# Layer 3 of a fused four-layer convolution kernel: row sums on VectorE, one mask operation for four heads, and other orders of columns in PSUM

## The chip, the cores and the metric

The kernel runs on one core of a Trainium2 chip. The metric is the device time of one execution in microseconds (us); a kernel's time is the median of its runs. Engines are named as in the profile: PE is the matmul engine, PEld its weight load, DVE is VectorE, ACT is ScalarE, POOL is GpSimd, SP is SyncE, whose queue issues nearly all DMAs in order.

## The reference, cut to what matters

The input `x` has 4 images of 256 channels, 48 x 48 pixels. Four layers follow each other, each of the form `x = x + layer(groupnorm(x))`. Layers 0 to 2 are convolutions, which the change does not touch. Layer 3 is a linear attention over boxes of pixels. It has 8 heads of 32 channels and three window sizes:

```python
q = sigmoid(Wq x); k = sigmoid(Wk x); v = (Wv x) / |Wv x| per head and pixel
Ik  = cumsum over rows and columns of k
Ikv = the same of the outer product of k and v
for w in (1, 2, 4):                      # boxes of side 48, 24 and 12
    wk, wkv = box(Ik), box(Ikv)          # sums of k and of k*v over the box around a pixel
    norm = sum_d q_d * wk_d
    outs.append((sum_d q_d * wkv_d) / (norm + 1e-6))
out = Wout concat(outs) + bout
```

A box sum is a difference of prefix sums along the columns and along the rows.

## The kernel before, in words

All of it is one program. A helper class `InOrder` records every operation in the order in which Python issues it, so nearly all rows of the profile carry the one line L244 and are told apart by tile names. Layers 0 to 2 fill the first 1390 us or so; the projections of layer 3 for image 0 already run in their shadow. Layer 3 is the rest.

**Blocks and tiles.** Layer 3 works through 48 blocks: 4 images, 2 halves of the channels (`ct`, four heads each), 6 blocks of 8 pixel rows (`rb`). A block goes through 8 to 12 score tiles; there are 480 in all. For a tile, `scores` computes on PE the products of queries and keys of four heads into two PSUM tiles `s` (a pair of heads each). `masked` makes the window masks of it in SBUF tiles `sm`: ACT and DVE write the widest window (a relu; PE has added large negative numbers where the window does not reach), DVE multiplies the middle window by a 0/1 mask, and POOL multiplies DVE's result by the mask of the narrowest window. `sums` multiplies the three with the values `vs` on PE, into three accumulators `acc`, one for each window. `LAG = 2`: while PE computes scores of tile n it sums tile n-2. Columns inside a block are stored `(w r)`: the pixel's column first, its row in the block of 8 second. Sums of a finished block are copied by ACT into `stage`.

**Norms.** A second path computes the denominators.
- `qk` projects q and k, takes the sigmoid on ACT into `sg`, and stores q in column order (`q_d`), k in two orders (`k_d` by way of a second tile `kt`, and `kf_d` in row order).
- `k_sums` runs twice side by side, once for each half of the channels, over 4 x 6 blocks of rows (48 steps in all). It loads the keys of 8 rows into `kp`, a tile with gaps of zeros between the rows, sums along the columns with two scans on DVE (`cs`), subtracts two shifted views for each window on DVE (`pt`), and then sums down the rows on POOL: eight adds of 3 windows x 48 columns, and a copy of the last row into `carry`. The result goes to DRAM (`kb_d`).
- `norms` loads two such rows of sums (`nhi`, `nlo`) and the queries (`nq`), and on POOL subtracts and multiplies, the queries read by a rearranged view. PE sums over the channels of each head into `norm_ps` (row order); ACT copies it into `ns`. It goes through DRAM (`n_d`, `nr`, the reciprocal on DVE, `r_d`).
- `prepare` loads the reciprocals, spread over channels, into `rc`, and POOL multiplies the first half's sums `o` by them. `finish` does the same for the second half on DVE (`stage`), multiplies by `Wout` on PE into `out_ps`, and DVE adds bias and residual into `res`. Both reciprocal products read `rc` by a rearranged view, and the addition of the residual writes `res` by one.

**What sets the order.** The side jobs (`qk`, `k_sums`, `norms`, `prepare`, `finish`, states of whole key blocks) are Python generators. After every tile `advance` lets them take steps. A planner gives each tile a budget of PE time and of POOL time: `pool_turn` holds a job back until the POOL budget allows it, by the cost `pool_op(n) = 190 + 1.95 n` ns; the budget of a tile is 3600 ns less `far_time`, the cost of its own narrow masks. Since all queues are in order, a side job that comes late on POOL holds up what stands behind it: mask products on POOL, loads on SP, norm matmuls on PE.

Of the kernel before, what the change touches and what calls it, by code (L numbers as in the profile page):

```python
# [247 lines left out]
def conv_preact_kernel(  # L248
# [71 lines left out]
    q_d = [dram.tile([C, HW], F32, tag=f"q{b}", name=f"q_d{b}") for b in range(B)]  # L320
    k_d = [dram.tile([C, HW], F32, tag=f"k{b}", name=f"k_d{b}") for b in range(B)]
# [105 lines left out]
    class Projection:  # L427
# [50 lines left out]
        def qk(self, g, a, name, mo):  # L478
            b = self.b
            while g not in self.xn:  # L480
                if g in self.left:
                    return
                yield 1
            yield from take("kt")
            yield from bank(1, NCT * product_time(NB))
            ps = self.ps_tile()[:, 0:NB]
            for ct in range(NCT):
                self.product(
                    ps,
                    proj[name][:, ct, mo * P : (mo + 1) * P],  # L490
                    self.xn[g][:, ct],
                    start=(ct == 0),
                    stop=(ct == NCT - 1),
                )
            self.used(g)
            t = self.scr.tile([P, NB], F32, tag="sg", name="sg")
            if name == "q":
                rows = t.rearrange("p (c x r) -> p c r x", c=NKC, x=KC)
            else:
                rows = t.rearrange("p (r c x) -> p c r x", c=NKC, x=KC)  # L500
            act.activation(
                rows, ps.rearrange("p (c r x) -> p c r x", c=NKC, x=KC), AF.Sigmoid
            )
            chans, cols = slice(mo * P, (mo + 1) * P), slice(a * NB, (a + 1) * NB)
            if name == "k":
                kt = self.scr.tile([P, NB], F32, tag="kt", name="kt")
                act.copy(kt.rearrange("p (c r x) -> p c r x", c=NKC, x=KC), rows)
            yield 1
            if name == "k":
                sync.dma_start(out=k_d[b][chans, cols], in_=kt)  # L510
            sync.dma_start(out=(q_d if name == "q" else kf_d)[b][chans, cols], in_=t)
            free["kt"] += 1
            made.add((name, b, mo, a))
# [1108 lines left out]
    with (  # L1622
# [4 lines left out]
        tc.tile_pool(name="smp", bufs=2 * (LAG + 1), reuse_waits="tile") as smp,  # L1627
# [27 lines left out]
        GAP = HALVES[0] + 1  # L1655
# [5 lines left out]
        carry = wts.tile([P, NCT, NW, W], F32, name="carry")  # L1661
# [10 lines left out]
        def k_sums(mo):  # L1672
# [14 lines left out]
            for at, (b, a) in enumerate(todo):  # L1687
# [3 lines left out]
                while step < loaded + FETCH + 1:  # L1691
                    yield 1
                yield from take("cs")
                cs = scr.tile([P, (RB + 1) * ROW], F32, tag="cs", name="cs", bufs=1)
                n = GAP + RB * ROW
                for i, j in ((0, n // 2), (n // 2, n)):
                    dve.tensor_tensor_scan(
                        cs[:, i:j],
                        kp[:, i:j],
                        kp[:, 0:1].to_broadcast([P, j - i]),  # L1700
                        cs[:, i - 1 : i] if i > 0 else 0.0,
                        ALU.add,
                        ALU.add,
                    )
                    yield 1
# [4 lines left out]
                for wi, h in enumerate(HALVES):  # L1710
                    dve.tensor_sub(pt[:, wi], shifted(cs, h - 1), shifted(cs, -h - 1))
                    yield 1
                free["cs"] += 1
                for r in range(RB):
                    if r % 2 == 0:
                        yield from pool_turn(NW * W, 2)
                    if a > 0 or r > 0:
                        up = pt[:, :, r - 1, :] if r > 0 else carry[:, mo]
                        pool.tensor_add(pt[:, :, r, :], pt[:, :, r, :], up)
                pool.tensor_copy(carry[:, mo], pt[:, :, RB - 1, :])  # L1720
                yield 1
# [8 lines left out]
        def norms(b, rb):  # L1730
# [4 lines left out]
            def load(ct):  # L1735
# [3 lines left out]
                qf = scr.tile([P, W, RB], F32, tag="nq", name="nq")  # L1739
                sync.dma_start(  # L1740
                    out=qf.rearrange("p w r -> p (w r)"),
                    in_=q_d[b][chans, rb * NB : (rb + 1) * NB],
                )
# [28 lines left out]
            for hi, lo, qf in loaded:  # L1772
                for wi, h in enumerate(HALVES):
                    n = min(RB, max(0, h + 1 - rb * RB))
                    if n < RB:
                        yield from pool_turn((RB - n) * W)
                        pool.tensor_sub(hi[:, wi, n:RB], hi[:, wi, n:RB], lo[:, wi, n:RB])
                for wi in range(NW):
                    yield from pool_turn(NB)
                    pool.tensor_mul(hi[:, wi], hi[:, wi], qf.rearrange("p w r -> p r w"))  # L1780
                sums.append(hi)
# [3 lines left out]
            for ct in range(NCT):  # L1785
# [3 lines left out]
                for wi in range(NW):  # L1789
                    pe.matmul(  # L1790
                        ps[D * wi : D * (wi + 1), 0:NB],
                        head_sel[:, ct, :],
                        sums[ct][:, wi].rearrange("p r w -> p (r w)"),
# [97 lines left out]
        class Block:  # L1891
# [48 lines left out]
            def masked(self, a, half, ss):  # L1940
# [9 lines left out]
                def room():  # L1950

                    t = smp.tile([P, SM_ROOM], F32, tag="sm", name="sm")
                    at, blocks_, views = 0, {}, {}
                    for wi in wis:
                        y0, y1 = rows_seen(wi, a, rb)
                        ps = self.parts(wi, a, half)
                        if wi == 0:
                            n = sum(p1 - p0 for _, p0, p1 in ps) * (y1 - y0)
                            block = t[:, at : at + 2 * n].rearrange("p (j n) -> p j n", j=2)
                            blocks_[wi] = block  # L1960
                            at, o = at + 2 * n, 0
                            for c, p0, p1 in ps:
                                m = (p1 - p0) * (y1 - y0)
                                views[wi, c] = block[:, :, o : o + m].rearrange(
                                    "p j (x r) -> p j x r", r=y1 - y0
                                )
                                o += m
                            continue
                        for c, p0, p1 in ps:
                            n = 2 * (y1 - y0) * (p1 - p0)  # L1970
                            views[wi, c] = t[:, at : at + n].rearrange(
                                "p (j x r) -> p j x r", j=2, r=y1 - y0
                            )
                            at += n
                    assert at <= SM_ROOM
                    return blocks_.get(0), views

                pairs = [room() for _ in ss]

                def times_mask(engine, wi, c, rows, cols, dst, src):  # L1980
# [5 lines left out]
                        dst, src, m.unsqueeze(1).to_broadcast([P, 2, ncol, nr])  # L1986
# [4 lines left out]
                def middle(s, room_):  # L1991
                    y0, y1 = rows_seen(1, a, rb)
                    for c, p0, p1 in parts_seen(1, half):
# [4 lines left out]
                        times_mask(dve, 1, c, (y0, y1), (p0, p1), room_[1][1, c], src)  # L1998

                def widest(engine, s, room_):  # L2000
                    n = room_[0].shape[2]
                    lo, hi = strip_columns(half) if full else (0, n)
                    if engine is act:
                        act.activation(room_[0], s[:, :, lo:hi], AF.Relu)
                    else:
                        dve.tensor_scalar_max(room_[0], s[:, :, lo:hi], 0.0)

                first, second = zip(ss, pairs)
# [8 lines left out]
                if many:  # L2017
                    (y0, y1), (z0, _) = rows_seen(2, a, rb), rows_seen(1, a, rb)
                    seen1 = {c: p0 for c, p0, _ in parts_seen(1, half)}
                    for _, views in pairs:  # L2020
                        for c, p0, p1 in parts_seen(2, half):
                            src = views[1, c][
                                :, :, p0 - seen1[c] : p1 - seen1[c], y0 - z0 : y1 - z0
                            ]
                            times_mask(pool, 2, c, (y0, y1), (p0, p1), views[2, c], src)
                return [views for _, views in pairs]
# [24 lines left out]
            def sums(self, wi, a, half, sms):  # L2051
# [3 lines left out]
                for k, (c, p0, p1) in enumerate(self.parts(wi, a, half)):  # L2055
                    for j in range(HG):
# [5 lines left out]
                            sms[j // 2][wi, c][:, j % 2],  # L2062
# [24 lines left out]
        def prepare(i):  # L2087
# [26 lines left out]
            for wi in range(NW):  # L2114
                yield from pool_turn(NB)
                ow = o[:, wi].rearrange("p (w r) -> p w r", w=W)
                pool.tensor_mul(ow, ow, rcs[0][:, wi].rearrange("p (r w) -> p w r", w=W))
# [4 lines left out]
        def finish(i, stage):  # L2122
# [13 lines left out]
            def divide(wi):  # L2136
                sw = stage[:, wi].rearrange("p (w r) -> p w r", w=W)
                dve.tensor_mul(sw, sw, rc[:, wi].rearrange("p (r w) -> p w r", w=W))
# [3 lines left out]
            for mo in range(NCT):  # L2142
                yield from bank(HOLD, NCT * product_time(NB))
                ps = ps_m.tile([P, 512], F32, tag="st", name="out_ps")[:, 0:NB]
                for wi in range(NW):
# [6 lines left out]
                    for t in range(NCT):  # L2152
                        kt = wi * NCT + t
                        tiled(
                            ps,
                            wout_sb[:, kt, mo * P : (mo + 1) * P],
                            os[t][:, wi, :],
# [4 lines left out]
                if mo == 0:  # L2162
                    free["rc"] += 1
                xs = res[:, mo].rearrange("p r w -> p w r")
                dve.scalar_tensor_tensor(
                    xs, ps.rearrange("p (w r) -> p w r", w=W), bout_sb[:, mo : mo + 1], xs, ALU.add, ALU.add
                )
# [111 lines left out]
        def far_time(i, a, half):  # L2279
# [4 lines left out]
            return 2 * sum(pool_op(2 * n) for n in columns(NW - 1, a, half, rb))  # L2284
# [79 lines left out]
```

## Time and profile before

| what | value |
|---|---|
| median of 3 runs | 3273.11 us (3265.43 to 3276.16) |
| the profiled execution | 3273.94 us, span 3272.1 us |
| mean granted PE clock | 0.955 of full speed |
| busy: PE, PEld | 2902.1 us (89%), 2004.4 us (61%) |
| busy: DVE, ACT, POOL | 2017.0 us (62%), 963.2 us (29%), 1613.6 us (49%) |
| instructions on DVE, ACT, POOL | 3907, 1894, 2658 |

The span runs from the first to the last instruction of the profiled execution. A row of a group reads: line, engine, operation, output tile <- input tiles, the most frequent shape of output <- input (and how many other shapes the group mixes), xcount | busy us in all, mean ns of one | idle us of the engine just before them, and what ended most of it. A row of the timeline gives the start, the duration, engine, operation and count, and in brackets the idle time before and what ended it. In rows of PE an f32 matmul counts twice, as it runs in two instructions.

### The profile page before, as it was taken

Reading aid. Unit: us, or ns where it says so; the run is one execution under the profiler, and the core shown is the slowest. Engines: PE = TensorE matmul, PEld = TensorE weight load, DVE = VectorE, ACT = ScalarE, POOL = GpSimd, SP = SyncE. Lnnn points to the kernel's source line nnn. Section 1 sums busy time; section 2 is a strip of 40 time slices with the busy share of each in tenths; the row PEclk is TensorE's granted clock in tenths of the full one; section 3 lists DMA queues with packets and bytes.
Section 4 is the critical chain, followed back from the end, with each engine's and each line's share of the span. In section 5 each row is a group of like instructions: output and inputs, shape, how many; then the busy total and the mean of one; then the engine's idle time right before and its main releaser. Section 6 shows DMA issues by size and latency. Waiting matters only on the chain.

```text
span 3272.1 us, 98025 instructions
## 1 busy us (share of the span) xinstructions
PE 2902.1 (89%) x41802; PEld 2004.4 (61%) x41802; DVE 2017.0 (62%) x3907; ACT 963.2 (29%) x1894; POOL 1613.6 (49%) x2658
## 2 busy tenths in 40 slices
PE   3678999899899978889986879998999999999999
PEld 2456777678677756756553536564656655666665
DVE  7886578648856632656675636665556665655555
ACT  0002210111121053245431224442335532333332
POOL 0000021003002130358999968989857888844554
PEclk9889899999999978989998989999999999999999
DMA  8746513332341243144554645354543354511322
GB/s 269 222 152 186 168 47 128 112 121 83 103 155 57 90 148 121 61 128 131 170 173 136 178 145 160 118 170 138 159 123 126 126 162 149 164 40 41 87 75 68
DMA packets 373126, 424.46 MB, mean 130 GB/s; under 512 B 129075, under 2 KB 328531, under 8 KB 371539
## 3 DMA queue, kind: packets, MB, share of 16 engines
q1 hardware_dynamic: 371491, 416.32, 41.1%
q8 instruction: 331, 5.42, 0.7%
q0 software_dynamic: 144, 1.08, 0.2%
q14 instruction: 104, 0.85, 0.1%
q10 hardware_dynamic: 1056, 0.79, 0.1%
HBM read 287.91 MB, written 131.25 MB: 128 GB/s over the span
## 4 chain that ended last, share of the span: by engine, by line
PE 51%; POOL 16%; DVE 10%; DMA 3%; ACT 3%; issue 3%; SPq 1%; ACTq 0%; POOLq 0%; DVEq 0%
PE cv L244 15%; PE s L244 13%; PE acc L244 11%; POOL sm L244 6%; PE out_ps L244 5%; PE proj_ps L244 4%; POOL nhi L244 4%; POOL pt L244 3%; PE ap L244 2%; DVE sm L244 2%; DVE l2v L244 2%; ACT sm L244 2%; SPq L244 1%; DVE v L244 1%; POOL vu L244 1%
## 5 line engine op out<-in xcount | busy, mean ns | idle before, releaser
L244 DVE TENSOR_TENSOR sm<-s,masks 128x448 f32<-128x448 f32 (+11 forms) x1536 | 632.6, 468 | 443.7 <-PE s L244 417.3
L244 POOL TENSOR_TENSOR sm<-sm,masks 128x352 f32<-128x352 f32 (+11 forms) x1024 | 685.9, 702 | 363.9 <-DVE sm L244 263.1
L244 ACT ACTIVATE sm<-s 128x384 f32<-128x384 f32 (+2 forms) x864 | 470.5, 545 | 845.3 <-PE s L244 662.2
L244 PE MATMUL acc<-sm,vs 128*32 128x128 f32 (+20 forms) x17920 | 626.1, 279 | 36.4 <-POOL sm L244 31.7
L244 PE MATMUL cv<-vx,wt 128*128 128x288 f32 x2080 | 562.8, 427 | 88.6 <-DVE vx L244 50.3
L244 PE MATMUL s<-qs,ks 32*128 32x192 f32 (+3 forms) x7680 | 594.3, 401 | 41.6 <-ACT sm L244 36.3
L244 PEld LDWEIGHTS acc<-sm,vs 128*32 128x32 f32 x17920 | 431.6, 110 | 241.9 <-issue 139.0
L244 PEld LDWEIGHTS s<-qs,ks 32*128 32x128 f32 x7680 | 372.7, 186 | 271.1 <-issue 122.3
L244 PEld LDWEIGHTS cv<-vx,wt 128*128 128x128 f32 x2080 | 404.7, 199 | 211.3 <-issue 52.7
L244 POOL MEMSET v<- 128x16 f32 (+1 forms) x120 | 18.7, 216 | 744.7 <-DVE vx L244 628.3
L244 PE MATMUL cv<-v,wl 128*128 128x384 f32 x1152 | 226.4, 357 | 25.2 <-DVE x L244 8.1
L244 PEld LDWEIGHTS cv<-v,wl 128*128 128x128 f32 x1152 | 216.4, 197 | 36.4 <-issue 16.7
L244 DVE TENSOR_SCALAR sm<-s 128x896 f32<-128x896 f32 (+1 forms) x96 | 111.1, 1157 | 186.1 <-PE s L244 161.2
L244 POOL TENSOR_TENSOR pt<-pt 128x144 f32<-128x144 f32 x336 | 188.0, 560 | 25.2 <-DVE pt L244 1.0
L244 POOL TENSOR_TENSOR nhi<-nhi,nq 128x384 f32<-128x384 f32 x144 | 176.2, 1243 | 0.0
L244 PE MATMUL s<-masks 24*128 24x192 bf16 (+2 forms) x1920 | 172.1, 269 | 0.0
L244 POOL TENSOR_TENSOR v<-l2v,v 128x384 fp32r<-128x384 f32 x96 | 109.0, 1166 | 117.4 <-ACT v L244 108.7
L244 PE MATMUL cv<-pad,wl 128*128 128x384 bf16 x864 | 145.6, 331 | 4.2 <-ACT pad L244 4.2
L244 PE MATMUL out_ps<-o,wout_sb 128*32 128x384 f32 x1152 | 123.8, 499 | 7.4 <-DVE res L244 3.4
L244 PE MATMUL out_ps<-stage,wout_sb 128*32 128x384 f32 x1152 | 123.5, 498 | 6.2 <-DVE stage L244 6.2
L244 PEld LDWEIGHTS <-wl 128*128 128x128 bf16 x864 | 84.5, 98 | 64.7 <-issue 7.2
L244 DVE SCALAR_TENSOR_TENSOR res<-out_ps,bout_sb,res 128x384 f32<-128x384 f32 x48 | 42.1, 878 | 128.9 <-PE out_ps L244 128.8
(174 smaller groups left out, 3515.1 us busy)
## 6 DMA issues: line engine op xcount, KB each, us to landing
wt<-wt SPq DMA_DIRECT2D x48, 768.0 KB
kb_d<-pt SPq DMA_DIRECT2D x48, 576.0 KB
rc<-r_d SPq DMA_DIRECT2D x192, 144.0 KB
nhi<-kb_d SPq DMA_DIRECT2D x120, 192.0 KB
nlo<-kb_d SPq DMA_DIRECT2D x88, 192.0 KB
o_d<-stage SPq DMA_DIRECT2D x24, 576.0 KB
o<-o_d SPq DMA_DIRECT2D x24, 576.0 KB
wl<-wl_d SPq DMA_DIRECT2D x16, 768.0 KB
```

Source lines behind the costliest of these rows:

```text
L244: return lambda *args, **kwargs: self.tc.keep_in_program_order(op(*args, **kwargs))
```

## The change

Four edits, all in layer 3:

1. `k_sums` sums down the rows first, on DVE and in place in `kp` (eight adds of 48 columns, and a copy of the last row into `carry`, which no longer has a window dimension). The scan multiplies the running sum by a tile `inside` that is 0 at the start of each row and 1 elsewhere, so that the sum starts anew in each row. The first columns of each window's result, where the window is cut at the border, are copied by ACT; the others are subtracted on DVE. The store follows at once, without a pause of a step.
2. `masked` gives the four heads of a tile one SBUF tile `sm` (3 buffers of double size instead of 6), and POOL multiplies the narrowest window of all four heads in one operation for each column part. `far_time` is adapted.
3. `qk` also stores q in row order (`qr_d`), by way of a copy on ACT into `kt`. `norms` loads this one, and multiplies without rearranging.
4. PE writes `norm_ps` in column order, through a rearranged view of its output, and `out_ps` in row order likewise. With this `rc`, `o`, `stage` and `res` are read and written without rearranged views.

The core of the diff:

```diff
@@ qk
-            if name == "k":
-                kt = self.scr.tile([P, NB], F32, tag="kt", name="kt")
-                act.copy(kt.rearrange("p (c r x) -> p c r x", c=NKC, x=KC), rows)
+            kt = self.scr.tile([P, NB], F32, tag="kt", name="kt")
+            pattern = "p (r c x) -> p c r x" if name == "q" else "p (c r x) -> p c r x"
+            act.copy(kt.rearrange(pattern, c=NKC, x=KC), rows)
...
+            first, second = (qr_d, q_d) if name == "q" else (k_d, kf_d)
+            sync.dma_start(out=first[b][chans, cols], in_=kt)
+            sync.dma_start(out=second[b][chans, cols], in_=t)
@@ set-up of layer 3
-        GAP = HALVES[0] + 1
+        GAP = HALVES[0]
...
+        inside = wts.tile([P, (RB + 1) * ROW], F32, name="inside")
+        nc.gpsimd.memset(inside, 1.0)
+        for r in range(RB + 1):
+            nc.gpsimd.memset(inside[:, r * ROW + GAP - 1 : r * ROW + GAP], 0.0)
@@ k_sums
+                keys = shifted(kp, 0)
+                for r in range(RB):
+                    if a > 0 or r > 0:
+                        up = keys[:, r - 1] if r > 0 else carry[:, mo]
+                        dve.tensor_add(keys[:, r], keys[:, r], up)
+                    if r % 4 == 3:
+                        yield 1
+                dve.tensor_copy(carry[:, mo], keys[:, RB - 1])
...
                     dve.tensor_tensor_scan(
                         cs[:, i:j],
+                        inside[:, i:j],
                         kp[:, i:j],
-                        kp[:, 0:1].to_broadcast([P, j - i]),
                         cs[:, i - 1 : i] if i > 0 else 0.0,
-                        ALU.add,
+                        ALU.mult,
                         ALU.add,
                     )
...
-                    dve.tensor_sub(pt[:, wi], shifted(cs, h - 1), shifted(cs, -h - 1))
+                    ahead_, behind_ = shifted(cs, h - 1), shifted(cs, 0)
+                    act.copy(pt[:, wi, :, : h + 1], ahead_[:, :, : h + 1])
+                    dve.tensor_sub(
+                        pt[:, wi, :, h + 1 :], ahead_[:, :, h + 1 :], behind_[:, :, : W - h - 1]
+                    )
                     yield 1
                 free["cs"] += 1
-                for r in range(RB):
-                    if r % 2 == 0:
-                        yield from pool_turn(NW * W, 2)
-                    if a > 0 or r > 0:
-                        up = pt[:, :, r - 1, :] if r > 0 else carry[:, mo]
-                        pool.tensor_add(pt[:, :, r, :], pt[:, :, r, :], up)
-                pool.tensor_copy(carry[:, mo], pt[:, :, RB - 1, :])
-                yield 1
@@ norms
-                    pool.tensor_mul(hi[:, wi], hi[:, wi], qf.rearrange("p w r -> p r w"))
+                    flat = hi[:, wi].rearrange("p r w -> p (r w)")
+                    pool.tensor_mul(flat, flat, qf)
...
-                        ps[D * wi : D * (wi + 1), 0:NB],
+                        ps[D * wi : D * (wi + 1), 0:NB].rearrange("p (w r) -> p r w", w=W),
@@ masked
-                    for _, views in pairs:
-                        for c, p0, p1 in parts_seen(2, half):
-                            src = views[1, c][
-                                :, :, p0 - seen1[c] : p1 - seen1[c], y0 - z0 : y1 - z0
-                            ]
-                            times_mask(pool, 2, c, (y0, y1), (p0, p1), views[2, c], src)
+                    for c, p0, p1 in parts_seen(2, half):
+                        src = views[1, c][:, :, p0 - seen1[c] : p1 - seen1[c], y0 - z0 : y1 - z0]
+                        times_mask(pool, 2, c, (y0, y1), (p0, p1), views[2, c], src)
@@ prepare
-                ow = o[:, wi].rearrange("p (w r) -> p w r", w=W)
-                pool.tensor_mul(ow, ow, rcs[0][:, wi].rearrange("p (r w) -> p w r", w=W))
+                pool.tensor_mul(o[:, wi], o[:, wi], rcs[0][:, wi])
@@ finish
-                sw = stage[:, wi].rearrange("p (w r) -> p w r", w=W)
-                dve.tensor_mul(sw, sw, rc[:, wi].rearrange("p (r w) -> p w r", w=W))
+                dve.tensor_mul(stage[:, wi], stage[:, wi], rc[:, wi])
...
-                            ps,
+                            ps.rearrange("p (r w) -> p w r", w=W),
                             wout_sb[:, kt, mo * P : (mo + 1) * P],
-                            os[t][:, wi, :],
+                            os[t][:, wi, :].rearrange("p (w r) -> p w r", w=W),
...
-                xs = res[:, mo].rearrange("p r w -> p w r")
-                dve.scalar_tensor_tensor(
-                    xs, ps.rearrange("p (w r) -> p w r", w=W), bout_sb[:, mo : mo + 1], xs, ALU.add, ALU.add
-                )
+                xs = res[:, mo].rearrange("p r w -> p (r w)")
+                dve.scalar_tensor_tensor(xs, ps, bout_sb[:, mo : mo + 1], xs, ALU.add, ALU.add)
@@ far_time
-            return 2 * sum(pool_op(2 * n) for n in columns(NW - 1, a, half, rb))
+            return sum(pool_op(4 * n) for n in columns(NW - 1, a, half, rb))
```

## The prediction

> **What bounds the kernel now.** Read the page's row of busy tenths first: layer 3, which the change touches, fills the span from about 1392 us on, with PE mostly at 9 and POOL mostly at 8 or 9 until about 2850 us. Which of the two sets the pace is told by cutting layer 3 into eight stretches of 60 score tiles each (equal attention work; eight batch halves). The cuts follow from the trace's score matmuls: 960 `s<-qs,ks` and 240 `s<-masks` per stretch. The view of busy time by stretch (us, then busy us and count for PE, PEld, DVE, ACT, POOL, then clock, DMA share, GB/s):
>
> ```profile
> 1392.20:1619.80 227.60, 213.49 (x4717) 137.76 (x4717) 144.61 (x295) 112.08 (x224) 180.66 (x340) 0.95 0.46 142
> 1619.80:1894.20 274.40, 229.07 (x4442) 135.43 (x4442) 174.64 (x305) 75.85 (x152) 255.36 (x362) 0.96 0.56 164
> 1894.20:2157.80 263.60, 238.14 (x4750) 139.85 (x4750) 145.55 (x288) 108.43 (x215) 216.41 (x352) 0.95 0.46 138
> 2157.80:2397.60 239.80, 218.56 (x4476) 134.58 (x4476) 138.94 (x264) 76.88 (x155) 208.35 (x301) 0.96 0.55 161
> 2397.60:2623.30 225.70, 221.02 (x4784) 135.76 (x4780) 140.33 (x284) 111.21 (x222) 167.31 (x326) 1.00 0.38 117
> 2623.30:2849.60 226.30, 212.38 (x4387) 133.87 (x4382) 134.86 (x258) 72.36 (x144) 197.94 (x271) 0.98 0.56 164
> 2849.60:3049.30 199.70, 186.89 (x4112) 127.84 (x4108) 104.78 (x215) 69.81 (x138) 96.39 (x155) 1.00 0.15 46
> 3049.30:3272.10 222.80, 210.78 (x4324) 131.50 (x4320) 117.77 (x235) 68.09 (x132) 114.37 (x162) 1.00 0.27 79
> ```
>
> The like stretches 3 and 5 (263.6 and 225.7 us, nearly the same PE count) and 2, 4 and 6 (274.4, 239.8, 226.3) differ by up to 48 us. The slow ones have the longest POOL time (255 us in stretch 2, 93%) and a lower clock (0.95 to 0.96 against 1.00)[...]. What PE waited for in layer 3, us in total, times, longest:
>
> ```profile
> PE s L244 <- ACT sm L244: 36.3, 94, 1.9
> PE acc L244 <- POOL sm L244: 31.7, 52, 2.1
> PE norm_ps L244 <- POOL nhi L244: 29.5, 18, 10.8
> PE norm_ps L244 <- DMA nhi<-kb_d: 8.6, 1, 8.6
> ...
> ```
>
> POOL stands behind most of it. The 10.8 us gap shows how, in the timeline: POOL's late `o` products free `rc`, SP's in-order queue waits there with its `rc` loads, the next norms' loads are issued behind them, POOL itself runs dry, and PE stands at its norm matmuls.
>
> ```profile
> 1911.96 2.33 POOL L244 TENSOR_TENSOR o<-o,rc 128x384 f32<-128x384 f32 x2
> ...
> 1914.70 2.12 SPq L244 DMA_DIRECT2D rc<-r_d  x3
> ...
> 1920.12 0.43 SPq L244 DMA_DIRECT2D nq<-q_d  x1
> ...
> 1925.31 0.99 POOL L244 TENSOR_TENSOR nhi<-nhi,nlo 128x384 f32<-128x384 f32 x1 [11.01 <-DMA nlo<-kb_d]
> ...
> 1928.97 3.77 PE L244 MATMUL norm_ps<-nhi,head_sel 128*32 128x384 f32 x6 [10.77 <-POOL nhi L244]
> ```
>
> So PE is the floor and POOL is what keeps the kernel off it until 2850 us.
>
> [...] partial-row `acc` matmuls that write 3 of every 8 columns start every 100 ns per eight at 57 columns (1.75 ns a column), the contiguous ones every 112 ns at 64 (1.75). [...] 1243 ns (`nhi*nq`) and 1244 ns (`o*rc`) with one operand strided, 1039 ns (`nhi-nlo`) with none, at 128x384. [...] the fastest `pt<-cs` took 541, the mean 743 beside POOL.
>
> **The change, part by part.** Groups of the page and of the trace by form carry these; counts after the change are those of the built order.
>
> (1) Row sums go from POOL to DVE, before the scan, on one copy of the keys instead of three windows.
>
> ```profile
> L244 POOL TENSOR_TENSOR sm<-sm,masks 128x352 f32<-128x352 f32 (+11 forms) x1024 | 685.9, 702 | 363.9 <-DVE sm L244 263.1
> ...
> L244 POOL TENSOR_TENSOR pt<-pt 128x144 f32<-128x144 f32 x336 | 188.0, 560 | 25.2 <-DVE pt L244 1.0
> L244 POOL TENSOR_TENSOR nhi<-nhi,nq 128x384 f32<-128x384 f32 x144 | 176.2, 1243 | 0.0
> ```
>
> POOL loses 188 us, 40 adds with `carry` at 543 ns (22) and 48 copies at 380 ns (18): -228. DVE gains 376 adds and 48 copies of 128x48. No such row exists; the line through DVE's `sm` rows (267 ns at 114, 619 at 448) gives 197 ns at 48[...]. I take 0.2 us: +85 (bounds 60 to 130, for a dependent chain). The scan keeps 2 x 300 elements (0.98 us each); its second operand is now a tensor instead of a broadcast, taken as equal, bound +-0.2 us x96. The three subtractions of 384 (743 ns) shrink to 184, 280 and 328 elements: [...], so -45. ACT copies the edges, 200, 104 and 56 elements: from `state` 238 ns at 96 and `kt` 512 at 384 about 0.34+0.25+0.20, times 48: +38. What queues behind the adds: they come in fours (0.8 us) between two tiles' mask products on DVE, which hold 2.2 us of a 3.5 us tile, so they fit; two key streams at once fill the tile. The store `kb_d<-pt` now follows its last subtraction directly, so SP's queue waits for DVE up to about 2 us, 48 times, in place of POOL.
>
> (2) One POOL operation for both pairs: 1024 become 512 of double size. The fixed part, from the means (518 ns at 130, 961 at 352: 2.0 ns per element), is 258 ns, from the medians (472, 886) 230. 512 x 0.235 = -120. The first now waits for both pairs' DVE products, about 1.1 us later than the first pair's, but PE takes both pairs of one column part before the next part, so it starts after one of two operations instead of three of four; two tiles of lag (7 us) cover it.
>
> (3) Rows and columns. `nhi*nq` and `o*rc` become contiguous: 0.2 us x (144+72) = -44 on POOL. DVE's `stage*rc` (1179 ns) [...]: -38 for 72; `res` (878 ns) to about 550, by the line above: -16 for 48. Row-ordered q costs 48 ACT copies at 512 ns (+25) and 48 stores of 192 KB on SP (0.4 us of issue each), beside PE. Twelve small POOL memsets at layer 3's start: +2.5 us.
>
> (4) PE writes `out_ps` and `norm_ps` with gaps[...]. Instructions and columns stay. Both together are about 222 us of PE: 2304 out matmuls in eights of 0.645 us (start to start, 186 us) and 48 norm sets of about 0.75 us. Price: 0 at best; nothing allows a gain. [...] f32 streams at 1.75 ns a column against 0.87 for the bf16 `acc<-zeros` matmuls[...]: I take 0.
>
> Sum: POOL -390 of 1437 us, 59% of the new layer 3; DVE -14 in all, but +0.8 us per key step where row sums run; ACT +63 (at 37%).
>
> **From POOL time to span.** With POOL off the path each stretch falls to PE's own time: odd ones to about 222 to 224 (stretch 5 has PE busy 221.0), even ones to 216 to 220 (stretch 6 has 212.4 plus the usual 2 to 3%). Gains: 5, 54, 40, 22, 4, 9, 1, 2 = 137 us. I take four fifths, as POOL still runs in bursts and DVE is fuller where keys are summed: -108. The profiled execution took 3273.94 (span 3272.1 and 1.8 around it), 0.8 over the median of the runs, 3273.11: 3274 - 108 = **3166**, range of this case alone 3110 to 3225.
>
> **Rivals.**
> A. POOL's relief is taken by another wait: DVE's adds before the masks hold back `s` (its wait on ACT/DVE is already 36 us), or SP waits on `kb_d<-pt`. For it: DVE 0.75 busy around stretch 2. Against: its sum falls. It leaves 15 to 60 of the 137: about 3235.
> B. Slower: gapped PSUM writes, in `finish` and `norms`. [...] against it the runs of three and the f32 rate. It decides from a factor of 108/222 = 0.49, 1.49 in all: at 1.5, 3277; at 2, 3166+222 = 3388.
> C. The edit does nothing: the order shows half the mask operations and no `pt` adds on POOL, so only if POOL's wait was never the limit; 3274.
>
> **Chances.** Main 0.63 (faster); A 0.18 (0.15 faster, 0.03 same); B 0.17 (0.15 slower, 0.02 same); C 0.02 (0.01 each). Within 0.3%, 10 us, a measurement here can't tell from no change. Faster 0.78, same 0.06, slower 0.16. The range 3105 to 3285 leaves out about 0.06 below and 0.08 to 0.1 above (most of B).
>
> **What would show it.** POOL near 1220 us in all, no `pt` row on POOL, 512 `sm` at about 1.15 us; `norm_ps` and `acc` waits on POOL below 25 us together; stretches 2 and 3 near 225 us with clock 0.98 or more. `out_ps` eights still at 645 ns start to start; 900 or more proves B. If POOL falls as said and stretches 2 and 3 stay over 250 us, A or C holds.

## The result, and the profile after

The changed kernel takes 3258.53 us (median of 6 runs, 3253.6 to 3261.18), the kernel before on the same chips 3271.72; the ratio is 0.9953, interval 0.9931 to 0.9974. That is faster by 0.5%, some 13 to 15 us, where the forecast was 108 us. The profiled execution took 3258.85 us, with a span of 3256.8.

POOL fell nearly as forecast (near 1220 us): the page has 1254.4 us for it instead of 1613.6. DVE, for which a fall of 14 us was forecast, rose: 2193.4 instead of 2017.0. These are some of the costliest groups, from the page of the changed kernel:

```profile
L244 POOL TENSOR_TENSOR sm<-sm,masks 128x704 f32<-128x704 f32 (+11 forms) x512 | 596.7, 1187 | 725.8 <-DVE sm L244 725.6
...
L244 DVE TENSOR_TENSOR kp<-kp 128x48 f32<-128x48 f32 x336 | 152.7, 455 | 9.7
...
L244 POOL TENSOR_TENSOR nhi<-nhi,nq 128x384 f32<-128x384 f32 x144 | 148.0, 1047 | 0.0
...
L244 PE MATMUL out_ps<-stage,wout_sb 128*32 128x384 f32 x1152 | 121.1, 491 | 10.4 <-DVE stage L244 10.3
```

The mask operation (1187 ns, half as many) and the query product (1047 ns instead of 1243) are near their forecasts. The row of `kp` is not: one add of 48 columns takes 455 ns on average, where the prediction's sum had 0.2 us.

The same eight stretches of 60 score tiles, in the view of busy time by stretch (columns as in the prediction), changed kernel:

```profile
1409.70:1648.30 238.60, 219.73 (x4719) 141.48 (x4718) 180.51 (x398) 125.91 (x266) 119.92 (x189) 0.94 0.48 150
1648.30:1904.00 255.70, 219.42 (x4442) 137.57 (x4438) 213.25 (x395) 81.62 (x187) 170.02 (x179) 0.93 0.55 157
1904.00:2165.40 261.40, 237.80 (x4727) 144.54 (x4724) 197.88 (x375) 119.49 (x251) 164.41 (x217) 0.94 0.53 162
2165.40:2383.60 218.20, 210.55 (x4508) 133.53 (x4508) 149.61 (x303) 81.91 (x174) 163.14 (x194) 1.00 0.60 176
2383.60:2616.90 233.30, 224.92 (x4786) 138.89 (x4782) 166.81 (x361) 124.30 (x256) 124.62 (x204) 0.99 0.39 124
2616.90:2834.90 218.00, 207.28 (x4383) 133.11 (x4382) 149.00 (x287) 74.44 (x158) 153.78 (x160) 0.98 0.59 169
2834.90:3033.80 198.90, 187.19 (x4114) 128.24 (x4110) 103.87 (x215) 69.75 (x138) 84.64 (x90) 1.00 0.15 47
3033.80:3256.80 223.00, 211.97 (x4320) 132.25 (x4320) 117.58 (x235) 67.92 (x132) 97.16 (x98) 1.00 0.26 78
```

Stretches 4 and 6 fell to PE's own time, as forecast (218 us). Stretches 2 and 3 stand at 255.7 and 261.4 us instead of near 225: POOL is busy for only two thirds of them, but DVE for 213 and 198 us, 22% and 36% more than before, and the clock is 0.93 and 0.94. Stretches 1 and 5 even grew, to 238.6 and 233.3 us (227.6 and 225.7 before), with DVE at 181 and 167 us instead of 145 and 140. Layer 3 as a whole takes 1847.1 us instead of 1879.9, a gain of 33; and it begins 17.5 us later (1409.7 instead of 1392.2), which takes half of that away again. The start itself moves by some 10 us from profile to profile; what belongs to the change is told with the experiments.

What PE waited for in layer 3 (us in total, times, longest):

```profile
PE s L244 <- ACT sm L244: 76.0, 103, 6.2
PE s L244 <- DVE sm L244: 13.1, 11, 2.9
PE out_ps L244 <- DVE stage L244: 10.3, 3, 6.2
```

POOL is gone from the head of the list; in its place the wait for the score buffers `s` rose from 37 us to 89. PE's only listed wait for POOL in this layer 3 is one of 1.6 us. One such gap of 6 us, in the timeline of the changed kernel:

```profile
1777.52 3.02 POOL L244 TENSOR_TENSOR sm<-sm,masks 128x704 f32<-128x704 f32 x2 [2.08 <-DVE sm L244]
1777.74 1.99 DVE L244 TENSOR_TENSOR_SCAN cs<-inside,cs,kp 128x300 f32<-128x300 f32 x1
...
1779.65 3.80 DVE L244 TENSOR_TENSOR kp<-kp 128x48 f32<-128x48 f32 x4
...
1780.50 1.94 POOL L244 TENSOR_TENSOR nhi<-nhi,nq 128x384 f32<-128x384 f32 x2
1782.40 2.89 POOL L244 TENSOR_TENSOR nhi<-nhi,nlo 128x384 f32<-128x384 f32 x3
1783.38 1.02 DVE L244 TENSOR_SCALAR nr<-nr 128x72 f32<-128x72 f32 x1
...
1784.94 1.07 DVE L244 TENSOR_TENSOR sm<-s,masks 128x224 f32<-128x224 f32 x4
...
1785.53 0.49 ACT L244 ACTIVATE sm<-s 128x384 f32<-128x384 f32 x1 [5.73 <-DVE sm L244]
...
1786.07 2.19 PE L244 MATMUL s<-qs,ks 32*128 32x192 f32 x16 [5.99 <-ACT sm L244]
```

A scan took 1.99 us and four adds 3.80 us, while POOL ran without a break; 1.6 us of work on a reciprocal (`nr`) followed. The mask products behind all this began at 1784.94. ACT's relu had waited 5.73 us for them, and PE 5.99 us for the relu.

**What stretches the operations of DVE.** The trace gives start and end of every instruction. The instructions of DVE are sorted here by how much of each lies beside running tensor_tensor instructions of POOL (layer 3 of the changed kernel; mean ns):

| on DVE | inputs | beside none | wholly beside POOL |
|---|---|---|---|
| `kp<-kp`, 48 columns | two in SBUF | 209 (164 of them) | 844 (97, longest 1527) |
| `kp<-kp,carry` | two in SBUF | 189 | 1034 |
| `carry<-kp`, a copy | one in SBUF | 176 | 836 |
| scan of 300, first and second | two in SBUF | 773, 832 | 1174, 1552 |
| `pt<-cs`, 184 | two in SBUF | 341 | 1057 |
| `stage<-stage,rc` | two in SBUF | 548 | 1349 |
| `sm<-s,masks`, 304 and 448 | one in PSUM, one in SBUF | 464, 618 | 464, 618 |
| `res<-out_ps,...` | one in PSUM, one in SBUF | 615 | 616 |

In each row with its inputs in SBUF the instructions took longer wholly beside POOL than beside none, from 1.5 times as long (the first scan) to 5.5 times (`kp<-kp,carry`); the copy, with one input, is among them. In the rows with one input in PSUM the two times agree to 1 ns. So an add of 0.2 us can be held for what is left of a POOL instruction: the mask operations took 0.80 to 1.70 us, as means by form, and the longest 2.10.

The ends of the instructions show the block itself. In the changed kernel 141 of the 336 adds took more than 260 ns, and each of them ended 62 to 72 ns after the end of a tensor_tensor instruction of POOL. In the six kernels of this document that keep these adds on DVE and were traced, there are 879 such adds, all with 60 to 72 ns. Longer instructions end later after POOL's end, by a step that fits their size: held subtractions of 184 columns after 203 to 213 ns, of 328 after 354 to 362, held `stage` products of 384 after 411 to 421, which is some 1.04 ns for each further column. Beside none the step is 1.05 ns (341 ns at 184 columns, 492 at 328). So a held instruction did its work from the end of POOL's instruction on, at its usual pace, and not slowly beside it.

This shows what DVE waits for, but not yet that PE's loss comes from it. Rivals were open: that the adds simply fill DVE, whatever POOL does, or that the four-head mask starts too late. The runs below separate these.

### The profile page after: what moved, and what is told of

Its sections match the earlier page's. It is cut to its first block, busy times and chain, and to the rows that moved or that the text cites. A ratio compares the mean times of both kernels' runs of the same rounds, so it can differ in the third digit from the quotient of the medians.

```text
span 3256.8 us, 97465 instructions
## 1 busy us (share of the span) xinstructions
PE 2897.6 (89%) x41802; PEld 2024.6 (62%) x41802; DVE 2193.4 (67%) x4331; ACT 1024.8 (31%) x2086; POOL 1254.4 (39%) x1732
## 4 chain that ended last, share of the span: by engine, by line
PE 59%; DVE 19%; ACT 5%; DMA 2%; issue 2%; POOL 1%; SPq 1%; ACTq 0%; DVEq 0%; POOLq 0%
PE s L244 16%; PE cv L244 15%; PE acc L244 14%; PE out_ps L244 5%; DVE sm L244 5%; PE proj_ps L244 4%; DVE kp L244 3%; PE ap L244 2%; ACT sm L244 2%; DVE l2v L244 2%; DVE cs L244 2%; DVE v L244 1%; PE keys_ps L244 1%; DVE k L244 1%; DVE x L244 1%
## 5 line engine op out<-in xcount | busy, mean ns | idle before, releaser
L244 POOL TENSOR_TENSOR sm<-sm,masks 128x704 f32<-128x704 f32 (+11 forms) x512 | 596.7, 1187 | 725.8 <-DVE sm L244 725.6
L244 PE MATMUL s<-qs,ks 32*128 32x320 f32 (+3 forms) x7680 | 620.2, 404 | 91.6 <-ACT sm L244 76.0
L244 PE MATMUL acc<-sm,vs 128*32 128x128 f32 (+20 forms) x17920 | 612.1, 281 | 3.6 <-issue 3.6
L244 PEld LDWEIGHTS s<-qs,ks 32*128 32x128 f32 x7680 | 388.2, 187 | 335.7 <-ACT sm L244 152.2
L244 DVE TENSOR_SCALAR sm<-s 128x896 f32<-128x896 f32 (+1 forms) x96 | 110.6, 1152 | 119.9 <-PE s L244 104.4
L244 PE MATMUL s<-masks 24*128 24x192 bf16 (+2 forms) x1920 | 183.0, 270 | 0.0
L244 DVE TENSOR_TENSOR kp<-kp 128x48 f32<-128x48 f32 x336 | 152.7, 455 | 9.7
L244 POOL TENSOR_TENSOR v<-l2v,v 128x384 fp32r<-128x384 f32 x96 | 108.4, 1159 | 120.5 <-ACT v L244 111.8
L244 POOL TENSOR_TENSOR nhi<-nhi,nq 128x384 f32<-128x384 f32 x144 | 148.0, 1047 | 0.0
L244 PE MATMUL ap<-seen,xT 120*128 120x120 f32 (+3 forms) x832 | 118.7, 302 | 0.0
```

Of the source, the lines that this page charges most:

```text
L244: return lambda *args, **kwargs: self.tc.keep_in_program_order(op(*args, **kwargs))
```

## Experiments

**The row adds back on POOL** (changed kernel, else as it is; eight adds of 48 columns instead of the old eight of 144):

```diff
+                    if r % 4 == 0:
+                        yield from pool_turn(W, 4)
...
-                        dve.tensor_add(keys[:, r], keys[:, r], up)
+                        pool.tensor_add(keys[:, r], keys[:, r], up)
...
-                dve.tensor_copy(carry[:, mo], keys[:, RB - 1])
+                pool.tensor_copy(carry[:, mo], keys[:, RB - 1])
```

> The changed kernel with one edit: the eight row sums of 48 columns and the copy into carry run on POOL instead of DVE, still before the scan. Theory L (lock): a DVE operation with two SBUF inputs waits while a POOL operation runs; this makes DVE the bound where keys are summed and holds back the reading of s, for which PE waits. It expects DVE busy 2193 -> about 1990 us, POOL 1254 -> about 1375 us, PE's waits for ACT and DVE at s together 89 -> below 50 us, time 3190 to 3215 us. Rival P (POOL's load alone sets the gain): POOL is given 120 us back, so slower than the changed kernel's 3258, 3265 or more. Rival S (the new ACT copies and SP stores are what hurts): no change, 3250 to 3260.

3182.23 us, ratio 0.9711 (0.9687 to 0.9735), better than the 3190 to 3215 expected. POOL is 127 us busier than in the changed kernel and the kernel 76 us faster. The adds in the view of one tile (ns min/median/max), with the first three stretches of this kernel:

```profile
L244 POOL TENSOR_TENSOR kp<-kp x336: 275/285/812, 1426.8 to 2604.6; 128x48 f32<-128x48 f32 x168
```

```profile
1407.60:1629.90 222.30, 213.82 (x4716) 137.64 (x4716) 145.45 (x292) 126.67 (x266) 151.74 (x292) 0.95 0.51 159
1629.90:1858.60 228.70, 213.34 (x4444) 134.19 (x4440) 168.72 (x298) 82.15 (x187) 200.30 (x279) 0.99 0.64 181
1858.60:2116.20 257.60, 228.18 (x4726) 137.31 (x4716) 155.20 (x296) 119.70 (x251) 187.73 (x296) 0.95 0.53 162
```

DVE in stretch 2 goes from 213 back to 169 us, and the stretch from 255.7 to 228.7. PE's wait for ACT at `s` is 30 us again. Stretch 3 stays long: PE's largest single wait there, 9.5 us, is for ACT's sigmoid `sg`. Layer 3 takes 1774.2 us: 106 less than before. A gain in layer 3 of the size that the prediction worked out is there once the adds are off DVE.

**The narrow mask left out** (POOL runs less, DVE's instructions are the same; the narrowest window is then summed from the middle window's scores, so its output is another):

```diff
-                        times_mask(pool, 2, c, (y0, y1), (p0, p1), views[2, c], src)
+                        views[2, c] = src
```

> The changed kernel without POOL's narrow mask product: the sums of the narrowest window read the middle window's masked scores, so that output differs and about 600 us of POOL work is left out; no DVE instruction is added or taken away, and the planner's order is unchanged. Theory L expects the mean of the DVE row adds to fall from 455 to below 320 ns, stage from 1106 to below 850 ns, DVE busy from 2193 to about 2080 us, time 3215 or less. Rival W (DVE just has too many instructions, whatever POOL does): row adds stay at 400 ns or more, time 3245 to 3260.

3177.23 us, ratio 0.9709 (0.9683 to 0.9734). The tile's view and groups by form, first of the changed kernel, then of this one:

```profile
L244 DVE TENSOR_TENSOR kp<-kp x336: 175/210/1527, 1427.6 to 2676.1; 128x48 f32<-128x48 f32 x168
```

```profile
L244 DVE TENSOR_TENSOR stage<-stage,rc 128x384 f32<-128x384 f32 x72 | 79.5, 1106 | 0.0
```

```profile
L244 DVE TENSOR_TENSOR kp<-kp x336: 177/209/1008, 1421.5 to 2595.4; 128x48 f32<-128x48 f32 x168
```

```profile
L244 DVE TENSOR_TENSOR kp<-kp 128x48 f32<-128x48 f32 x336 | 112.1, 334 | 9.7
...
L244 DVE TENSOR_TENSOR stage<-stage,rc 128x384 f32<-128x384 f32 x72 | 47.4, 661 | 0.0
```

The same 376 adds are on DVE, and its layer-3 time falls from 1417 to 1259 us, with POOL at 498 us instead of 1109. (Layer-3 times of DVE and POOL here and below are durations added up. Records of an engine overlap a little at their edges, so these sums are larger than the busy times of the view by stretch, which give DVE 1101 us before and 1279 after the change, POOL 1437 and 1078.) The list of PE's waits in the changed kernel has none for a mask product of POOL, so the gain does not come from PE's own path through POOL. The adds alone don't hold PE; adds beside POOL do. The mean of 334 ns just misses the forecast of below 320: some adds still meet POOL's other work (99 of 336 took more than 260 ns).

**Four heads undone to two** (the other three edits stay; `masked`, `smp`, `far_time` as before):

```diff
+                    for _, views in pairs:
+                        for c, p0, p1 in parts_seen(2, half):
...
+            return 2 * sum(pool_op(2 * n) for n in columns(NW - 1, a, half, rb))
```

> The changed kernel with the mask part undone: one POOL operation for each pair of heads, 1024 of half the size, six sm buffers. Theory L: the time in which POOL runs grows by 90 to 120 us, but each operation is half as long; waiting per DVE operation is about the length of a POOL operation times the chance of meeting one, so row adds at 380 to 450 ns, time 3245 to 3270. Rival P: POOL's load counts, 3280 or more. A rival within L, that only long POOL operations hurt: row adds below 330 ns and time below 3240.

3221.68 us, ratio 0.9839 (0.9818 to 0.9861): more time on POOL (1328.0 us), and 37 us faster than the changed kernel. That is better than the 3245 to 3270 expected. It lies where the second rival had it, that only long POOL instructions hurt, but that rival had the adds below 330 ns, and their 389 ns are in the main range. So the edit that saves time on POOL costs time here, and DVE's rows, by form, are shorter without it:

```profile
L244 DVE TENSOR_TENSOR kp<-kp 128x48 f32<-128x48 f32 x336 | 130.2, 389 | 9.6
...
L244 DVE TENSOR_TENSOR stage<-stage,rc 128x384 f32<-128x384 f32 x72 | 55.0, 766 | 0.0
```

**The four-head operation cut in two by columns.** It starts no earlier than in the changed kernel, after both pairs, but each instruction is half as long:

```diff
-                        times_mask(pool, 2, c, (y0, y1), (p0, p1), views[2, c], src)
+                        pm = (p0 + p1) // 2
+                        for q0, q1 in ((p0, pm), (pm, p1)):
+                            cut = slice(q0 - p0, q1 - p0)
+                            times_mask(
+                                pool, 2, c, (y0, y1), (q0, q1), views[2, c][:, :, cut], src[:, :, cut]
+                            )
```

> The changed kernel with each four-head mask operation on POOL cut in two by columns: 1024 operations of half the length, each still behind both pairs' DVE products, same tiles, same planner costs. It tells why one operation for each pair was 37 us faster than one for both. Theory L (length of a POOL operation is what DVE waits for): row adds 360 to 420 ns, DVE near 2100, time 3215 to 3235. Rival (the four-head operation starts later or its tile is held longer): as the changed kernel, 3250 or more, as POOL also works 100 us more.

3216.03 us, ratio 0.9837 (0.9811 to 0.9862), in its range and 42 us faster than the changed kernel (38 by the ratios). So it is the length of one POOL instruction, and neither its late start nor the tile that four heads share, as both stay. The mean of the adds missed its forecast of 360 to 420 ns:

```profile
L244 DVE TENSOR_TENSOR kp<-kp x336: 172/424/944, 1420.6 to 2635.9; 128x48 f32<-128x48 f32 x168
```

```profile
L244 DVE TENSOR_TENSOR kp<-kp 128x48 f32<-128x48 f32 x336 | 150.6, 449 | 9.6
...
L244 DVE TENSOR_TENSOR stage<-stage,rc 128x384 f32<-128x384 f32 x72 | 58.3, 812 | 0.0
```

POOL has 98 us more work in layer 3, so more adds met it (207 took more than 260 ns, instead of 141) and none waited long (at most 944 ns instead of 1527). The carry copies (579 to 403 ns), `pt` (715 to 587 on average) and `stage` (1106 to 812) gained; DVE's layer 3 falls by 70 us.

**`k_sums` as before** (the other edits stay):

```diff
-                        dve.tensor_add(keys[:, r], keys[:, r], up)
...
+                        pool.tensor_add(pt[:, :, r, :], pt[:, :, r, :], up)
```

> The changed kernel with the key sums as they were before (row sums of three windows on POOL after the subtractions); masks for four heads and the other column orders stay. Theory L: DVE loses its row adds, POOL gets 228 us back and stands at about 1480, 130 below the kernel before; time 3200 to 3235. Rival P: POOL's work sets the time, and 130 of the 360 us of relief is left: between the two kernels, 3262 to 3268. Rival S: ACT's edge copies are gone too, so no more than 10 us under the changed kernel.

3215.98 us, ratio 0.9819 (0.979 to 0.9847), in the range of 3200 to 3235. POOL has 1481.7 us, 227 more than in the changed kernel, and the kernel is faster by 43.

**The edits one at a time, on the kernel before.** Sums alone, masks alone, orders alone (edits 3 and 4 of the change), and sums with masks:

```diff
# sums alone
+                        dve.tensor_add(keys[:, r], keys[:, r], up)
# masks alone
+                    for c, p0, p1 in parts_seen(2, half):
# orders alone
+            first, second = (qr_d, q_d) if name == "q" else (k_d, kf_d)
```

> The kernel before with the key sums alone changed (row sums of 48 columns on DVE before the scan, ACT's edge copies); masks by pair and the column orders as before. Theory L (a DVE operation with two SBUF inputs waits for the POOL operation that runs): POOL 1613 -> about 1385 us, row adds on DVE at 400 to 480 ns, DVE 2017 -> about 2170, time 3225 to 3262. Rival P (POOL's load sets the time, DVE's waits cost nothing): below 3220.

> The kernel before with one POOL mask operation for both pairs alone. POOL 1613 -> about 1500 us. Theory L: POOL operations of up to 1.6 us hold DVE's subtractions and stage products longer (pt 743 -> 850 to 950 ns, stage 1179 -> 1250 or more), DVE grows by 20 to 50 us, though DVE has room here; time 3225 to 3255. Rival P: POOL's 110 us come through by more than a third, below 3235, with pt and stage as before. A rival that the longer operations hurt in every setting: 3272 or more.

> The kernel before with the column orders alone (q stored a second time by row, norms written by column and outputs by row in PSUM, products without rearranged views); key sums and masks as before. Expected: out matmuls still 645 ns per eight start to start, POOL about 44 us less, DVE about 50 us less, ACT +25 us, layer 3 shorter by 15 to 40 us and the part before it about 10 us longer, as ACT's ten more copies stand on the path there; time 3245 to 3268. Rival B (gapped PSUM writes slow PE): out matmuls above 800 ns per eight and time above 3290.

> The kernel before with the key sums and the four-head masks, column orders as before. Alone they gave 41 and 51 us. Theory L (DVE's two-input operations wait for the POOL operation that runs; long POOL operations and many such DVE operations multiply): the two don't add, row adds at 450 ns or more, DVE at or above 2180 us, layer 3 itself 1840 to 1865 us, time 3230 to 3255. Rival A (the gains add, and what spoils the sum of all three is the column orders with their ACT copies): 3175 to 3195.

With the runs above, all eight combinations are measured. L3 is layer 3 of the profiled execution, from its first score matmul to the end; DVE and POOL are their durations in it, added up (us):

| edits | median us | ratio (interval) | L3 starts, lasts | DVE | POOL | `kp` adds, `stage` ns |
|---|---|---|---|---|---|---|
| none | 3271.72 | 1 | 1392.2, 1879.9 | 1222 | 1496 | –, 1179 |
| sums | 3231.21 | 0.987 (0.9852–0.9888) | 1386.7, 1840.4 | 1366 | 1269 | 412, 1092 |
| masks | 3220.42 | 0.9828 (0.9803–0.9853) | 1387.2, 1831.3 | 1265 | 1405 | –, 1238 |
| orders | 3255.04 | 0.9948 (0.9931–0.9965) | 1411.2, 1845.2 | 1184 | 1441 | –, 854 |
| sums + masks | 3256.84 | 0.9962 (0.9949–0.9974) | 1397.0, 1865.2 | 1455 | 1167 | 492, 1301 |
| sums + orders | 3221.68 | 0.9839 (0.9818–0.9861) | 1404.1, 1812.6 | 1324 | 1204 | 395, 766 |
| masks + orders | 3215.98 | 0.9819 (0.979–0.9847) | 1408.6, 1813.8 | 1238 | 1343 | –, 992 |
| all | 3258.53 | 0.9953 (0.9931–0.9974) | 1409.7, 1847.1 | 1417 | 1109 | 478, 1106 |

(The `kp` column has the adds with `carry` in it.) By the ratios, each edit gains alone: 43, 56 and 17 us, 116 together, near the forecast of 108. Most of the loss lies in one pair: sums and masks together leave 12 of their 99, while the other two pairs leave 53 of 60 and 59 of 73. Sums bring 376 adds and 48 copies to DVE, masks make POOL's instructions twice as long. Masks alone ended just under its range, as the rival P had it; but P had `pt` and `stage` unchanged, and `pt` rose from 743 to 909 ns and `stage` from 1179 to 1238. Sums with masks ended 2 us over its range; sums alone and orders alone lie in theirs. Orders alone started layer 3 by 19 us later, where about 10 were expected.

**Rows on POOL and masks by pair** (the first and third experiment together):

> The changed kernel with the row sums on POOL and, besides, one mask operation for each pair of heads again. Theory L: DVE still has two-input operations (subtractions, scans, stage products), which meet POOL operations half as long, so pt, cs and stage are each 50 to 150 ns shorter than with row sums on POOL alone (760, 738, 865; 1097, 1225; 987 ns); but POOL works some 100 us more and stands above 0.95 in two stretches. Time within 12 us of row sums on POOL alone (3182). Rival P: POOL counts, 3200 or more. Rival, that shorter POOL operations always win as they did with row sums on DVE (37 us): 3165 or less.

3180.63 us, ratio 0.971 (0.969 to 0.9729), not to be told from 3182.23, as expected: without the adds on DVE the choice of mask no longer shows in the time. Shorter POOL instructions still cut DVE's layer-3 time (1159 us instead of 1221), but POOL has 99 us more; whether the two cancel or neither counts, no run shows.

**The ten early copies of q on POOL** (on the kernel with rows on POOL). Row-ordered q starts layer 3 later: at 1386.7 to 1397.0 us in the four profiles without it, at 1400.0 to 1411.2 in the eight with its copies all on ACT. About 10 us of that lie between 1118 and 1281 us of the kernel before (163.5 us there, 173.3 in the changed kernel), where the projections of image 0 run; ACT has ten copies of q more there.

```diff
-            act.copy(kt.rearrange(pattern, c=NKC, x=KC), rows)
+            copy = pool.tensor_copy if name == "q" and b == 0 else act.copy
+            copy(kt.rearrange(pattern, c=NKC, x=KC), rows)
```

> The changed kernel with the row sums on POOL, and besides the row-ordered copies of the first image's q (12, in the shadow of the layers before) on POOL, which is 20% busy there, instead of ACT. If ACT's ten more copies between 1118 and 1281 us are what starts layer 3 later, layer 3 starts 8 to 15 us earlier than with row sums on POOL alone (1407.6 us), and the time is 3165 to 3177. If the later start is chance or the stores' doing: 3178 to 3186.

3179.26 us, ratio 0.9723 (0.9696 to 0.9749), not to be told from 3182.23, and in the range of the rival (3178 to 3186), not in that of the copies (3165 to 3177). The same piece of work in the view by stretch, first with the copies on ACT (kernel with rows on POOL), then on POOL:

```profile
1123.00:1297.90 174.90, 136.10 (x598) 102.78 (x597) 47.72 (x135) 83.08 (x152) 35.08 (x119) 0.81 0.47 147
```

```profile
1124.00:1288.00 164.00, 130.70 (x601) 98.88 (x599) 48.17 (x129) 69.19 (x135) 41.56 (x124) 0.84 0.46 139
```

The piece is 11 us shorter, with ACT at 69 instead of 83 us, but most of that was lost again before layer 3, which started at 1404.6 us instead of 1407.6, where 8 to 15 us were expected. In the time of the kernel the effect is not shown.

**All of it: rows on POOL, masks by pair, early q copies on POOL.**

> Row sums on POOL, one mask operation for each pair of heads, and the first image's row-ordered q copied on POOL: the three edits that helped or did no harm. Theory L expects what the parts gave: 3181 (row sums on POOL, masks by pair) less 3 to 10 us for the copies, so 3168 to 3180 us, layer 3 itself 1765 to 1778 us.

3175.32 us, ratio 0.9688 (0.9662 to 0.9713), in its range: faster than both kernels, by 3.1% and, by the two ratios, some 2.7%. Layer 3 starts at 1396.6 us in its profile and takes 1780.9 us, just over the 1765 to 1778 expected.

## Why the prediction was wrong

**The step that failed is the price of DVE's adds in part (1)**, "I take 0.2 us: +85 (bounds 60 to 130)". It put the wait for POOL at nothing. The price holds for an add beside an idle POOL (209 ns), but 141 of the 336 waited for a POOL instruction to end. Measured: 336 adds at 455, 40 with `carry` at 670 and 48 copies at 579 ns, 207 us in all. Three other terms were too small for the same reason, as they left out the wait or took it from the kernel before with its shorter POOL instructions: the subtractions, 2.15 us a step where the forecast of -45 left 1.29 (+41; the line through DVE's `sm` rows, 267 ns at 114 columns and 619 at 448, gives 1.28, an estimate); `stage*rc`, 1106 ns where the -38 left about 650 (+33); the scans, 1108 ns on average instead of 980 (+12). Together with the +122 of the adds that is 208 us; the forecast of -14 becomes +194, and DVE's durations in layer 3 did rise by 195 us, from 1222 to 1417.

The trace before had the warning, and the prediction wrote it down: the fastest `pt<-cs` 541 ns, the mean "743 beside POOL". Those 200 ns on an instruction with two SBUF inputs went into the subtractions that the change takes away and by half into `stage*rc` (about 650 ns, where the same line gives 552, an estimate). The adds and the new subtractions were priced without them.

**Rival A happened**, at the place it named: DVE's adds ahead of the masks hold back `s`. Its sign came too: POOL fell, and stretches 2 and 3 stayed over 250 us. It was given 0.18, because DVE's "sum falls"; that sum was made with the wrong price. Its size for layer 3 was right (33 us remain, within "15 to 60"); not its total of 3235, as the later start was missing.

**"They come in fours (0.8 us) ... so they fit"** fell with it: four took 3.80 us in the gap shown, more than a tile's 3.5 us.

**Part (2)** was right on POOL (1187 ns, forecast 1.15 us) and had no term for what a longer POOL instruction does to DVE. Alone the edit gains 56 us; on top of sums and orders it loses 37 by the medians.

**Part (3)** was right on POOL: `nhi*nq` 1047 and `o*rc` 1031 ns, 0.2 us less each. `res` came to 615 ns (forecast 550). The ACT copies "beside PE" were not so for image 0, where that piece of the work is 10 us longer with them on ACT than before, and 11 us shorter again with them on POOL. The rest of the later start, up to 8 us ahead of that piece, remains open: layer 3's first sigmoid starts between 1151 and 1161 us in the four profiles without row-ordered q and between 1156 and 1164 in the ten with it.

**Part (4)** was right: eight `out_ps` matmuls (2304 in the trace for the 1152 f32 products that the program issues) start every 645 ns with gapped writes as with contiguous ones, and in each kernel a norm set that runs without a wait has its six starts within 0.34 us. Rival B, for which no trace had spoken, falls: f32 writes with steps of 8 and 48 columns were not slower here. Rival C, that POOL's wait was never the limit, falls with the 106 us that layer 3 gains once the adds are back on POOL.

**From POOL time to span**: 137 us of room, four fifths of it taken. With rows on POOL layer 3 gained 106, so the room was real and the size of this step held; what it assumed, that no other engine would be late, did not hold for the change as it was made.

## What to carry to other kernels

An instruction's price on DVE depended here on what POOL did beside it when its inputs lay in SBUF (an add of 48 columns: 209 ns beside none, 844 wholly beside POOL). Price such an instruction with the mean of a row of that kind beside POOL, not with the shortest or with a line through rows that have an input in PSUM. The longest wait grew with the length of POOL's instructions (adds of up to 1527 ns with masks for four heads, up to 933 and 944 with masks half as long), and the mean fell with the time that they ran (455 ns with POOL at 1109 us in layer 3, 334 with 498). Small two-input work in front of what PE waits for was better left on POOL itself here (313 ns on average there, in the last kernel of the experiments, against 455 on DVE). The table suggests that an input in PSUM would do as well, as mask products took the same 464 and 618 ns beside POOL, but no run tried it. Two edits that each gained lost most of it together (sums and masks: 43 and 56 us alone, 12 as a pair, by the ratios), as one multiplies the waiters and the other lengthens the wait; such a pair is measured as a pair.

## What the runs showed of the hardware that was not expected

- The block goes by instruction: each of the 879 adds over 260 ns, in six kernels, ended 60 to 72 ns after an instruction of POOL ended. An add of 0.2 us took 0.84 us on average when it lay wholly beside POOL, up to 1.53. Mask products with one input in PSUM kept their 464 and 618 ns beside POOL.
- A plain copy with one SBUF input was held too (176 against 836 ns; the 26 that took more than 230 ns ended 42 to 48 ns after a POOL instruction).
- Halving POOL's mask instructions, at 98 us more of POOL time, made the kernel 42 us faster.
- Adds of 48 columns took 313 ns on average on POOL (the last kernel of the experiments; 285 at the median with rows on POOL), against 560 for those of 144 before.
